# One of seven exponential-tile additions per attention step, moved from VectorE to GpSimd

## The chip, the cores and the metric

The kernel runs on one core of one Trainium2 chip. A core has a matrix engine (TensorE, "PE" in the profile, with its weight loads as "PEld"), VectorE ("DVE"), ScalarE ("ACT"), GpSimd ("POOL"), and a queue engine ("SP") that issues most of the transfers. The metric is the device time of one execution in microseconds; lower is better. Each engine works through its own instructions in order, and waits on semaphores for the results of others.

## What is computed

Two graph layers are applied to `x` of shape (16, 1024, 256), all in float32. The change lies in the softmax attention of the first layer, for 16 batches of 1024 nodes and 4 heads of 64 columns:

```python
g = relu(einsum('bcn,bnm->bcm', fea, Wg) * para)        # Wg from adj and column means
q = transpose(g).reshape(B, N, h, hd).transpose(0, 2, 1, 3)
kv = (x @ kv_w)...                                       # k, v per head
attn = softmax(einsum('bhnd,bhmd->bhnm', q, k) * scale, axis=-1)
out = einsum('bhnm,bhmd->bhnd', attn, v)
```

Around it stand layer norms, a residual sum, and a second layer (`A_hat @ features`, two linear maps with batch norms).

## The kernel before

Everything lies in `fast_path`. The order of the instructions on every engine is the order in which they are written (`tc.manual_schedule` for all five engines), so an instruction that has to wait holds up all that follows on its engine.

**The batch loop.** For each of the 16 batches `b`, TensorE does: the attention of `b`; the graph products of batch `b + 1` (`graph` for batch 1, `graph_seven` from batch 2 on, which uses seven products in place of eight); its keys and values; and the first linear map of the second layer for batch `b` (`linear1_all`). After the last batch a second stage does the other linear map, the batch norms and the output.

**One attention step.** `attention` has 4 steps per batch, 64 in all: two halves of 512 queries (`g`) by two pairs of heads (`pair`). `scores(s)` makes 8 tiles (`m` = 0..7): TensorE multiplies keys by queries into PSUM (`f_s`, L743; three such PSUM buffers), ScalarE takes the exponential into an SBUF tile `p` of 128 x 1024 floats (`f_p`, L751; 8 buffers). `values(s)` then multiplies `p` by `v` (`f_o`, L793; one PSUM bank), and VectorE moves the bank out by a transposition (L806).

**The sums of the softmax.** The denominators come from adding up the 8 tiles `p` on VectorE, in two chains: `acc` takes tiles 0, 1, 4, 6 and `flat` (the tile named `f_sums`) takes 2, 3, 5, 7. The additions in their order are L757 (`acc` = p0 + p1), **L763 (`flat` = p2 + p3)**, L766 four times (p4 to `acc`, p5 to `flat`, p6 to `acc`, p7 to `flat`), and L771 (`acc` + `flat`). These are the seven additions. Then `partial(s)` transposes `acc` into the tile of `flat` (L777) and reduces it (L785), and L806 follows after the values. In the VectorE queue the order of one step is therefore L757, L763, L766 x4, any step of `hooks`, L771, L777, L785, L806.

**What else hangs in these queues.** In steps 0 and 1 a hook makes the graph weights of the next batch: ScalarE L353 and L356, VectorE `masked` (L361). In step 2 the reciprocals of the first half are made (L826 to L829) and applied (L844). Right behind the last L806 of a batch come, on VectorE, the remaining `masked` (L361) for graph weights 2 to 7, mixed with the sums that `graph_seven` needs (L557, L561, L564, L569), the reciprocals of the second half (L826 to L829), and L844. TensorE meanwhile does the first two plain products (L514) and then the seven-product scheme (L576), of which `m2(2)` uses graph weight 7.

**Buffers.** `flat` is one buffer (tag "sums", one of one) that is also used by `graph_seven` for a loaded tile of sums; `acc` has two. The sums tile of the next step may be written only when L785 of this step has read it. GpSimd holds, in the whole kernel, the powers of the norms (L260), some DMA issues (L482, L496, L379) and sixteen small additions and products in the first batch (L1273, L1274). In the four attention steps of batch 8 it runs nothing (0.00 us).

Of the kernel before, what the change touches and what calls it, by code (L numbers as in the profile page):

```python
# [29 lines left out]
def fast_path(  # L30
# [20 lines left out]
    nc = tc.nc  # L51
# [124 lines left out]
    with ExitStack() as stage:  # L176
# [555 lines left out]
        def attention(b, qT, kT, v, hooks):  # L732

            steps = [(g, pair) for g in range(NH) for pair in range(HEADS // 2)]
            p_of, acc_of, odd_of, oT_of, o_of, red_of = {}, {}, {}, {}, {}, {}

            def scores(s, within=None, before_last=()):
                g, pair = steps[s]
                for m in range(NC):
                    ps = ps_s.tile([P, 2, 512], F32, tag="s", name=f"f_s_{b}_{s}_{m}")  # L740
                    for e in range(2):
                        rows_e = slice(e * HD, (e + 1) * HD)
                        nc.tensor.matmul(  # L743
                            ps[:, e, :],
                            kT[rows_e, pair, ts(m, P)],
                            qT[rows_e, pair, ts(g, 512)],
                            start=True,
                            stop=True,
                        )
                    p = pp.tile([P, 2, 512], F32, tag="p", name=f"f_p_{b}_{s}_{m}")  # L750
                    nc.scalar.activation(p, ps, AF.Exp)  # L751
                    p_of[s, m] = p
                    if m == 1:
                        acc = pp.tile(
                            [P, 2, 512], F32, tag="acc", name=f"f_acc_{b}_{s}", bufs=2
                        )
                        nc.vector.tensor_add(acc, p_of[s, 0], p)  # L757
                        acc_of[s] = acc
                    elif m == 3:
                        odd = ow.tile([P, 2, 16, 32], F32, tag="sums", name=f"f_sums_{b}_{s}")  # L760
                        odd_of[s] = odd
                        flat = odd.rearrange("p e j i -> p e (j i)")
                        nc.vector.tensor_add(flat, p_of[s, 2], p)  # L763
                    elif m > 3:
                        to = flat if m % 2 else acc_of[s]
                        nc.vector.tensor_add(to, to, p)  # L766
                    if m == 5 and within:
                        within()
                for step in before_last:
                    step()  # L770
                nc.vector.tensor_add(acc_of[s], acc_of[s], flat)  # L771
# [105 lines left out]
            for i in range(len(steps)):  # L877
                scores(
                    i,
                    collect if i == 2 else None,  # L880
                    [*hooks.get(i, ()), *([invert, spread] if i == 2 else [])],
                )
                partial(i)
                if i == 2:
                    scale()
                values(i)
# [1492 lines left out]
```

## Time and profile before

| what | value |
|---|---|
| three runs, median (lowest to highest) | 2392.19 us (2390.81 to 2392.27) |
| the profiled execution's own time | 2392.53 us |
| its span in the profile | 2390.7 us |
| granted TensorE clock, mean | 0.996 |
| PE busy, share of span | 2351.4 us, 98% |
| DVE busy | 1953.6 us, 82% |
| ACT busy | 1345.3 us, 56% |
| POOL busy | 174.9 us, 7% |
| one batch in the middle (from the attention of batch 8 to that of batch 9) | 130.82 us |

A row of the timeline gives the start in microseconds from the start of the span, the length, the engine, the line of the kernel, the operation, output and inputs by name, and their shapes; at its end in brackets the idle time of the engine before it, and what ended it. A row of the weight loads ("PEld") tells when TensorE took up the next operand, and on whom it waited. The sum of the lengths of VectorE's rows is a little more than the time that they take, because one addition begins while the one before is still draining: additions of 1.22 us start 1.13 to 1.14 us apart.

### The profile page before, as it was taken

The page shows a single profiled execution, that of the slowest core. Times are in us where ns is not written, and L with a number is a line of the kernel's source. Part 1 is how long each engine was busy: PE and PEld are TensorE (multiplying, and loading weights), DVE is VectorE, ACT ScalarE, POOL GpSimd, SP SyncE. Part 2 cuts the span into 40 slices and gives each one's busy share as a digit, 9 for nine tenths or more (in the row PEclk, how much of TensorE's full clock was granted, in tenths as well). Part 3 has the DMA queues.
Part 4 walks back from the last instruction along what each step waited for, and adds up shares of the span by engine and source line. Part 5 has one row for each costly group of instructions (what it writes and reads, how often), then busy time and mean ns, then how long its engine had stood idle before and what let it go on. Part 6 is the DMA issues. An engine that isn't in the chain of part 4 may idle for free.

```text
span 2390.7 us, 24368 instructions
## 1 busy us (share of the span) xinstructions
PE 2351.4 (98%) x7950; PEld 1032.3 (43%) x7950; DVE 1953.6 (82%) x2806; ACT 1345.3 (56%) x1974; POOL 174.9 (7%) x253
## 2 busy tenths in 40 slices
PE   8999999999999999999999999999999999999995
PEld 4443444434343434444343434344444434444444
DVE  6788888797979798897979797988978797757766
ACT  6846555564736455555647374555555565346653
POOL 2030010101010000101010100001010100000000
PEclk9999999999999999999999999999999999999998
DMA  5042433433342434334333424242433321355579
GB/s 189 7 144 93 142 119 123 137 118 90 99 152 68 161 93 158 102 124 136 121 99 107 141 62 163 89 167 93 138 122 123 117 83 53 114 210 181 175 238 376
DMA packets 178649, 312.44 MB, mean 131 GB/s; under 512 B 33616, under 2 KB 117072, under 8 KB 178512
## 3 DMA queue, kind: packets, MB, share of 16 engines
q1 hardware_dynamic: 164176, 267.25, 33.5%
q0 software_dynamic: 9728, 26.76, 3.7%
q10 hardware_dynamic: 4608, 16.78, 1.7%
q8 instruction: 65, 1.06, 0.2%
q14 instruction: 72, 0.59, 0.1%
HBM read 195.04 MB, written 96.79 MB: 122 GB/s over the span
## 4 chain that ended last, share of the span: by engine, by line
PE 97%; DMA 1%; DVE 1%; issue 0%; ACT 0%; SPq 0%; DVEq 0%; ACTq 0%; POOLq 0%; POOL 0%
PE f_s L743 19%; PE f_o L793 19%; PE f_aps L952 16%; PE f_zps L1058 6%; PE f_gps L576 6%; PE f_vps L450 5%; PE f_gpsx L576 5%; PE f_gps L514 4%; PE f_zx L1596 4%; PE f_zm L1596 3%; PE f_kpsx L691 2%; PE f_gps L404 2%; PE f_kps L691 2%; PE f_z2ps L1534 1%; PE f_outps L1819 1%; PE f_zps L1140 1%
## 5 line engine op out<-in xcount | busy, mean ns | idle before, releaser
L751 ACT ACTIVATE f_p<-f_s 128x1024 f32<-128x1024 f32 x512 | 477.4, 1048 | 190.3 <-PE f_s L743 190.1
L743 PE MATMUL f_s<-f_qT,f_kT 64*128 64x512 f32 x2048 | 457.2, 596 | 0.0
L793 PE MATMUL f_o<-f_p,f_v 128*64 128x512 f32 x2048 | 453.6, 595 | 0.0
L743 PEld LDWEIGHTS f_s<-f_qT,f_kT 64*128 64x128 f32 x2048 | 190.1, 185 | 264.6 <-ACT f_p L751 119.0
L793 PEld LDWEIGHTS f_o<-f_p,f_v 128*64 128x64 f32 x2048 | 141.4, 137 | 304.3 <-issue 264.4
L353 ACT ACTIVATE f_w<-f_row,f_col 128x1024 f32<-128x1024 f32 x127 | 147.0, 1157 | 38.8 <-PE f_gps L514 26.9
L766 DVE TENSOR_TENSOR f_acc<-f_acc,f_p 128x1024 f32<-128x1024 f32 x128 | 155.9, 1218 | 4.2 <-ACT f_p L751 4.2
L361 DVE SCALAR_TENSOR_TENSOR f_w<-f_w,f_adj 128x1024 f32<-128x1024 f32 x127 | 152.8, 1212 | 7.5 <-ACT f_w L356 7.3
L766 DVE TENSOR_TENSOR f_sums<-f_sums,f_p 128x1024 f32<-128x1024 f32 x128 | 155.8, 1217 | 0.0
L260 POOL TENSOR_TENSOR f_rstd_b<-f_var_b,f_mhalf 128x4 f32<-128x4 f32 (+1 forms) x31 | 33.1, 1069 | 1496.0 <-DVE f_var_b L259 1496.0
L356 ACT ACTIVATE f_w<-f_w 128x1024 f32<-128x1024 f32 x127 | 134.4, 1058 | 4.0
L952 PE MATMUL f_aps<-f_ahatT,f_hs 128*128 128x512 f32 x256 | 115.1, 592 | 0.0
L952 PE MATMUL f_aps<-f_ahatT,f_h_b 128*128 128x512 f32 x256 | 113.4, 596 | 0.0
L450 PE MATMUL f_vps<-f_kvw,f_hT 128*128 128x256 f32 x512 | 113.1, 379 | 0.0
L952 PE MATMUL f_aps<-f_t,f_hs 128*128 128x512 f32 x256 | 112.5, 592 | 0.0
L281 ACT ACTIVATE f_h_b<-f_x,f_shift_b,f_rstd_b 128x256 f32<-128x256 f32 x128 | 66.3, 592 | 75.8 <-DVE f_shift_b L266 75.6
L450 PEld LDWEIGHTS f_vps<-f_kvw,f_hT 128*128 128x128 f32 x512 | 97.3, 190 | 20.1 <-issue 7.7
L281 ACT ACTIVATE f_h_a<-f_x,f_shift_a,f_rstd_a 128x256 f32<-128x256 f32 x126 | 73.8, 587 | 50.7 <-DVE f_shift_a L266 50.7
L757 DVE TENSOR_TENSOR f_acc<-f_p,f_p 128x1024 f32<-128x1024 f32 x64 | 76.8, 1200 | 28.4 <-ACT f_p L751 28.4
L514 PE MATMUL f_gps<-f_w,f_h_a 128*128 128x512 f32 x224 | 99.9, 599 | 0.0
L763 DVE TENSOR_TENSOR f_sums<-f_p,f_p 128x1024 f32<-128x1024 f32 x64 | 78.3, 1223 | 21.8 <-ACT f_p L751 21.8
L777 DVE STREAM_TRANSPOSE f_sums<-f_acc 128x1024 f32<-128x1024 f32 x64 | 79.7, 1245 | 2.2
(278 smaller groups left out, 3607.5 us busy)
## 6 DMA issues: line engine op xcount, KB each, us to landing
f_t<-ft SPq DMA_DIRECT2D x84, 512.0 KB, 11.0
fz<-f_z SPq DMA_DIRECT2D x64, 512.0 KB, 9.7
f_x<-in_x_dram SPq DMA_DIRECT2D x31, 1024.0 KB, 7.4
f_zb<-fz SPq DMA_DIRECT2D x42, 512.0 KB, 4.2
f_att<-f_oT SPq DMA_DIRECT2D x512, 32.0 KB, 1.9
fx<-f_x SPq DMA_DIRECT2D x16, 1024.0 KB, 4.4
fhT<-f_hQ POOLq DMA_DIRECT2D x112, 128.0 KB, 2.9
f_hT<-fhT SPq DMA_DIRECT2D x28, 512.0 KB, 5.8
```

The source lines that it names most:

```text
L353: nc.scalar.activation(w, rows[b], AF.Abs, bias=cols[b][:, c : c + 1], scale=0.5 / C)
L361: nc.vector.scalar_tensor_tensor(w, w, 1.0, adj_t[c], ALU.subtract, ALU.mult)
L450: nc.tensor.matmul(ps[:, i, :], hT[e][:, ts(c4 + i, P)], kvw_t[:, e, C : 2 * C], start=(e == 0), stop=(e == CC - 1),)
L514: nc.tensor.matmul(gps[d][:, ts(g, 512)], h[:, c, ts(d, P)], w[:, ts(g, 512)], start=(c == 0), stop=(c == PLAIN - 1),)
L576: nc.tensor.matmul(ps, left, right, start=fresh and n == 0, stop=(n == PAIRS - 1), skip_group_check=more,)
L743: nc.tensor.matmul(ps[:, e, :], kT[rows_e, pair, ts(m, P)], qT[rows_e, pair, ts(g, 512)], start=True, stop=True,)
L751: nc.scalar.activation(p, ps, AF.Exp)
L766: nc.vector.tensor_add(to, to, p)
L793: nc.tensor.matmul(o_of[s][e * HD : (e + 1) * HD, :], v[:, m, ts(2 * pair + e, HD)], p[:, e, :], start=(m == 0), stop=(m == NC - 1),)
L952: nc.tensor.matmul(ps, left[:, m, :], right(m), start=not more and m == 0, stop=(m == KH - 1), skip_group_check=more,)
L1058: nc.tensor.matmul(ps[i], left[:, ts(i, P)], right, start=not more, stop=True, skip_group_check=more,)
L1596: nc.tensor.matmul(ps, left[:, m, :], right[:, m, :], start=start and m == 0, stop=(m == 1), skip_group_check=not start,)
```

## The change

In each of the 64 attention steps the addition of tiles 2 and 3 is issued on GpSimd's queue in place of VectorE's. The output tile, the operands and the four additions that follow on the two chains are the same. The L766 of `m == 5` (p5 to `flat`), which came behind L763 on the same engine, now waits for GpSimd's result.

```diff
                     elif m == 3:
                         odd = ow.tile([P, 2, 16, 32], F32, tag="sums", name=f"f_sums_{b}_{s}")
                         odd_of[s] = odd
                         flat = odd.rearrange("p e j i -> p e (j i)")
-                        nc.vector.tensor_add(flat, p_of[s, 2], p)
+                        nc.gpsimd.tensor_add(flat, p_of[s, 2], p)
```

## The prediction

> **What bounds the kernel now.** I first read the page: busy shares and the chain that ended last.
>
> ```profile
> PE 2351.4 (98%) x7950; PEld 1032.3 (43%) x7950; DVE 1953.6 (82%) x2806; ACT 1345.3 (56%) x1974; POOL 174.9 (7%) x253
> ...
> PE 97%; DMA 1%; DVE 1%; issue 0%; ACT 0%; SPq 0%; DVEq 0%; ACTq 0%; POOLq 0%; POOL 0%
> ```
>
> TensorE is the chain for 97% of the span. A busy PE could hide waits, so next the busy times by stage of one middle batch: four attention steps of batch 8, the graph products of batch 9, the rest.
>
> ```profile
> 1115.97:1172.31 56.34, 56.34 (x257) 20.75 (x257) 53.31 (x55) 41.40 (x50) 0.00 (x0) 1.00 0.21 65
> 1172.31:1197.48 25.17, 25.17 (x59) 11.13 (x60) 21.54 (x36) 10.54 (x17) 0.97 (x1) 1.00 0.75 270
> 1197.48:1246.79 49.31, 49.31 (x133) 24.09 (x131) 36.15 (x74) 21.13 (x42) 8.44 (x13) 1.00 0.32 103
> ```
>
> The columns after the length are PE, PEld, DVE, ACT, POOL, clock, DMA share and GB/s. TensorE has no gap in any stage; GpSimd does nothing in the attention; but VectorE is busy 53.31 of 56.34 us there, so it has only 3 us in hand per batch. Batches repeat every 130.82 us, and from 65.5 to 2052 us TensorE is never idle: its 39.3 us of idle time lie before the first attention (10.3) and after the last (29.3, less 0.3 of rounding). So taking work off VectorE can win nothing here; the question is only whether VectorE gets late enough to hold TensorE up. For that I read the timeline of VectorE through the last two steps of batch 8 and into the graph products, and the weight loads beside it.
>
> ```profile
> 1147.22 1.22 DVE L757 TENSOR_TENSOR f_acc<-f_p,f_p 128x1024 f32<-128x1024 f32 x1 [0.96 <-ACT f_p L751]
> 1149.05 1.23 DVE L763 TENSOR_TENSOR f_sums<-f_p,f_p 128x1024 f32<-128x1024 f32 x1 [0.61 <-ACT f_p L751]
> 1150.19 1.22 DVE L766 TENSOR_TENSOR f_acc<-f_acc,f_p 128x1024 f32<-128x1024 f32 x1
> ...
> 1161.82 1.18 DVE L757 TENSOR_TENSOR f_acc<-f_p,f_p 128x1024 f32<-128x1024 f32 x1
> 1163.19 1.22 DVE L763 TENSOR_TENSOR f_sums<-f_p,f_p 128x1024 f32<-128x1024 f32 x1 [0.19 <-ACT f_p L751]
> 1164.34 1.22 DVE L766 TENSOR_TENSOR f_acc<-f_acc,f_p 128x1024 f32<-128x1024 f32 x1
> ...
> 1172.67 0.70 DVE L806 STREAM_TRANSPOSE f_oT<-f_o 128x512 f32<-128x512 f32 x1
> ...
> 1185.94 1.22 DVE L361 SCALAR_TENSOR_TENSOR f_w<-f_w,f_adj 128x1024 f32<-128x1024 f32 x1
> ```
> ```profile
> 1187.37 0.19 PEld L576 LDWEIGHTS f_gps<-f_w,f_h_a 128*128 128x128 f32 x1 [0.24 <-DVE f_w L361]
> 1187.80 0.19 PEld L576 LDWEIGHTS f_gps<-f_w,f_h_a 128*128 128x128 f32 x1 [0.24 <-issue]
> ```
>
> From 1163.19 to 1191.7 VectorE has no idle time. The last graph weight (`masked` 7, L361) is ready at 1185.94 + 1.22 = 1187.16, and TensorE takes it up at 1187.37, for a product that begins at 1187.79. A load takes 0.19, so it could come as late as 1187.60: **about 0.4 us of slack** (0.44 less a little for the semaphore). This is the tightest place; the earlier products of L576 have 2 us or more.
>
> **What the Trainium skill says.** "SBUF — State Buffer", section "Who interferes with whom": a VectorE instruction with two SBUF inputs contends with a GpSimd instruction that reads SBUF, over a read interface that they share, and the second to issue blocks until the first is done. Both L757 and L766 have two SBUF inputs, as has the moved addition. The trace of before can't confirm it: POOL is at 0.00 us in the attention window. "GPSIMD Engine Reference", section 3.1: a float32 addition of 2048 columns takes 4497 ns on GpSimd, 2293 ns on VectorE. VectorE's 1.22 us for 1024 columns fits the latter (half is 1.15, plus a fixed part); GpSimd shows only 128 columns:
>
> ```profile
> L1273 POOL TENSOR_TENSOR f_unused_d<-f_ahatT,f_ident 128x128 f32<-128x128 f32 x8 | 4.7, 588 | 17.9 <-ACT f_unused_r L1260 17.9
> L1274 POOL TENSOR_TENSOR f_ahatT<-f_ahatT,f_ident 128x128 f32<-128x128 f32 x8 | 4.4, 546 | 0.6
> ```
>
> **The price of the moved addition, P.** Low end: half of the page's 4497 ns, 2.25 us. High end: the trace's 546 ns for 128 columns times 8, 4.4 us, which counts its fixed part eight times. Taking the page's slope (2.17 ns per column, its 2.6 cycles at 1.2 GHz) off the 546 ns leaves about 0.27 us fixed, so 2.22 + 0.27 = 2.49; I take **P = 2.4 us**, between that and 2.25.
>
> **The change, part by part.** Removed: 64 VectorE additions at a pitch of 1.135 us (the start-to-start distance around L766), 73 us of VectorE time, none of it on TensorE's path. Added: 64 GpSimd additions, on a queue with nothing else in the attention, so nothing is held up behind them; GpSimd's DMA issues (L482, L496) come in the later stage. They start when exponential 3 is there and L785 of the step before has freed `flat`; L785 is long done. Added too: the wait of L766 for p5; behind it stand all of VectorE's queue down to L806 and `masked`. Its semaphore costs nothing while P is served first, since under the lock VectorE has already been stopped for it.
>
> With the lock, L757, the GpSimd addition and the next L766 go one after another, whichever comes first; so each step costs VectorE P - 1.135 = 1.27 us more, less what idle time it swallows. Walking batch 8 (idle times from the timeline; by "late" I mean against before):
> - Step 0: no idle. The first L766, at 1123.20 before, is 1.27 late.
> - Step 1: L757 starts at 1133.20 + 1.27 = 1134.47, frees the port 1.13 later, GpSimd until 1138.0; L766 stood at 1136.11: 1.9 late (0.58 idle swallowed).
> - Step 2: L757 without its 0.96 idle at 1146.26 + 1.9 = 1148.16; GpSimd from 1149.29 to 1151.69; L766 stood at 1150.19: 1.5 late, and 1.2 after a 0.29 wait further on.
> - Step 3: L757 at 1161.82 + 1.2 = 1163.0; GpSimd from 1164.15 to 1166.55; L766 stood at 1164.34: **2.2 late**.
>
> No step delays TensorE inside the attention: `values` of step 1 needs L806 of step 0, done 3.8 us ahead; those of steps 2 and 3 have 5.0 and 3.4 us in hand. But L806 of step 3, and `masked` 7 behind it, come 2.2 late; less 0.4 of slack, TensorE stalls **1.8 us per batch**. Then VectorE catches up: at 1193.85 it waits 2.18 us for ScalarE anyway. The transfer that waits for L785 (L528, 3.6 us to landing) has some 4 us in hand.
>
> Fourteen batches (1 to 14) have this shape: 14 x 1.8 = 25.2. Batch 7 has no idle in steps 1 and 2 and ends 3.5 late: +1.3. Batch 9 has 0.36 of idle in place of 0.19 in its last step: -0.2. Batch 0: its `masked` wait 0.69, 0.90 and 0.90 us for ScalarE, which covers it: 0. Batch 15: the sum L937 ends at 2057.82 and is wanted at about 2059.0; about 1.95 late less 1.2: +0.7. Sum: **+27 us**. The profiled execution took 2392.5 (span 2390.7 plus 1.8 around it, 0.3 above the median of 2392.19): 2392.5 + 27.0 = **2419.5 us**.
>
> P counts four times in a batch: 0.1 us more of it is 0.4 x 14 = 5.6 us. P = 2.25 gives 2411, P = 2.6 gives 2431, and hand-overs at the lock count like P. If the engines share the port, so that the block is worth 2.0 us, step 3 ends 0.8 late: 14 x 0.4, about 2398.
>
> **The rivals.**
> - *No contention, and the add fits* (ends on the other side: same). VectorE gains 1.135 us in steps 0 to 2 and idles. In step 3 exponential 3 is ready at 1163.1; GpSimd would end at 1165.6, and the L766 for p5 stood at 1165.47: 0.1 to 0.2 late, under the slack of 0.4. Time 2392.5. It decides if additions on both engines overlap at full speed and P stays below about 2.7. For it: nothing in this trace shows a lock. Against: the page names this very pair of operations.
> - *No contention, but a slow add.* Then only the last step counts: late by P - 2.3, less 0.4. P = 3.3 gives 14 x 0.6, 2401; P = 4.4 gives 14 x 1.7, 2416. For it: 546 ns for 128 columns. Against: half of the page's figure.
> - *Faster.* VectorE would have to end a wait of TensorE in the attention; there is none.
>
> **How the numbers follow.** The lock, whole or partial: 0.76, most of it between 2398 and 2440. Slow add: 0.07. No contention and same: 0.14. Faster by some effect that I don't see: 0.03. A measurement tells about 0.2% (4.8 us) from no change, so faster 0.03, same 0.14, slower 0.83. The range from 2397 to 2440 takes in a weak lock and P up to about 2.75; it leaves out no change, faster, and a lock with larger hand-overs.
>
> **What would show it.** Right: VectorE's L757 or first L766 stretched to 2 to 3.5 us, or started late, beside the POOL row; L806 of step 3 about 3.3 us after TensorE's first L514 where it ended 1.1 after it before; a PE wait on L361 of about 1.8 us in 14 batches and a batch period of about 132.6 us. GpSimd's own spans are rough ("Perfetto Trace Analysis", section "GPSIMD Engine Instruction", advises against trusting them), so P is best read from when the L766 for p5 starts. Wrong: L766 at 1.22 us beside GpSimd, or a period of 130.82.

## The result, and the profile after

The changed kernel takes 2404.85 us (median of 6 runs, 2403.97 to 2405.18) against 2391.79 us before (6 runs): a ratio of 1.0054, 95% interval 1.0041 to 1.0067. It is 13 us slower; 27 had been forecast. The direction, the mechanism and the place were as predicted, the size was half.

The page of the changed kernel, with the line of busy times and the chain that ended last (profiled execution 2403.97 us, span 2402.2 us):

```profile
PE 2353.6 (98%) x7950; PEld 1031.8 (43%) x7950; DVE 1982.7 (83%) x2742; ACT 1347.2 (56%) x1974; POOL 351.4 (15%) x317
...
PE 78%; DVE 11%; issue 5%; ACT 3%; DMA 2%; SPq 1%; DVEq 0%; ACTq 0%; POOLq 0%; POOL 0%
```

VectorE has 64 instructions less and is busy 29 us *more*. The chain no longer runs through TensorE alone: it now leaves it for VectorE and ScalarE once per batch. The stages of batch 8 (columns as before: length, PE, PEld, DVE, ACT, POOL, clock, DMA share, GB/s) say where:

```profile
1121.53:1177.87 56.34, 56.34 (x257) 20.76 (x257) 53.72 (x50) 41.41 (x50) 11.13 (x4) 1.00 0.20 64
1177.87:1204.00 26.13, 25.37 (x59) 11.15 (x60) 23.02 (x37) 10.65 (x17) 1.02 (x1) 1.00 0.71 260
1204.00:1253.30 49.30, 49.30 (x132) 24.07 (x131) 36.17 (x74) 21.14 (x42) 8.43 (x13) 1.00 0.34 104
```

The attention takes 56.34 us as before, the last stage too. Only the graph products have grown, and there TensorE has its gap: 26.13 - 25.37 = 0.76 us. The table of TensorE's waits names one new cause between 190 and 2060 us, 14 times:

```profile
PE f_gps L576 <- DVE f_w L361: 10.6, 14, 0.8
```

(Three single waits of 0.3 to 0.7 us that the trace of before lacks lie outside that stretch, in the loads and in the last stage. Run 2 below, in which nothing was moved to GpSimd, has two of them as well, and in the third TensorE waits for a transfer of a weight, L1303.) The end of graph weight 7 and TensorE's rows at that place, in batch 8:

```profile
1193.00 1.22 DVE L361 SCALAR_TENSOR_TENSOR f_w<-f_w,f_adj 128x1024 f32<-128x1024 f32 x1
```
```profile
1192.50 1.02 PE L576 MATMUL f_gpsx<-f_w,f_h_a 128*128 128x512 f32 x2
1194.28 1.12 PE L576 MATMUL f_gps<-f_w,f_h_a 128*128 128x512 f32 x2 [0.76 <-DVE f_w L361]
```

This is `m2(2)`, which waits for graph weight 7. The idle time of 0.76 us understates the loss, because TensorE's rows overlap: this product begins 1.78 us behind the one ahead of it, where it began 0.86 us behind it before (1186.93 to 1187.79). From one batch's first graph product to the next the kernel now takes 131.77 us instead of 130.82: 0.95 us more in each of 14 batches, 13.3 us, which is the difference of the medians (13.1). (The two profiled spans differ by 11.5 only: this execution reached the first attention 1.06 us earlier than before's, and from the attention of batch 15 to the end it took 0.56 us less.)

Then the two engines in the attention of batch 8: VectorE in the first and the last step, and below it GpSimd in all four:

```profile
1126.50 1.21 DVE L757 TENSOR_TENSOR f_acc<-f_p,f_p 128x1024 f32<-128x1024 f32 x1
1127.82 3.20 DVE L766 TENSOR_TENSOR f_acc<-f_acc,f_p 128x1024 f32<-128x1024 f32 x1
1130.94 1.21 DVE L766 TENSOR_TENSOR f_sums<-f_sums,f_p 128x1024 f32<-128x1024 f32 x1
...
1168.13 1.18 DVE L757 TENSOR_TENSOR f_acc<-f_p,f_p 128x1024 f32<-128x1024 f32 x1
1169.67 2.95 DVE L766 TENSOR_TENSOR f_acc<-f_acc,f_p 128x1024 f32<-128x1024 f32 x1 [0.36 <-ACT f_p L751]
1172.54 1.21 DVE L766 TENSOR_TENSOR f_sums<-f_sums,f_p 128x1024 f32<-128x1024 f32 x1
```
```profile
1126.49 3.44 POOL L763 TENSOR_TENSOR f_sums<-f_p,f_p 128x1024 f32<-128x1024 f32 x1 [12.80 <-ACT f_p L751]
1140.57 2.60 POOL L763 TENSOR_TENSOR f_sums<-f_p,f_p 128x1024 f32<-128x1024 f32 x1 [10.64 <-ACT f_p L751]
1154.65 2.36 POOL L763 TENSOR_TENSOR f_sums<-f_p,f_p 128x1024 f32<-128x1024 f32 x1 [11.48 <-ACT f_p L751]
1168.80 2.73 POOL L763 TENSOR_TENSOR f_sums<-f_p,f_p 128x1024 f32<-128x1024 f32 x1 [11.79 <-ACT f_p L751]
```

GpSimd begins its row beside L757, waits for it inside its row (3.44 against 2.36 in the third step, where nothing was in its way) and ends at 1129.93. L766 begins at 1127.82 and lasts 3.20 us, to 1131.02: it is stopped until GpSimd is done and then needs 1.09 us. The same rows of step 0 before the change:

```profile
1120.94 1.21 DVE L757 TENSOR_TENSOR f_acc<-f_p,f_p 128x1024 f32<-128x1024 f32 x1
...
1124.34 1.22 DVE L766 TENSOR_TENSOR f_sums<-f_sums,f_p 128x1024 f32<-128x1024 f32 x1
```

All 64 first L766 are stretched like this (their group, with the later additions to `acc`, has a mean of 2035 ns where it had 1218). The second L766, the one that has the new semaphore to wait for, stays at 1.21 to 1.22 in every case, and begins 1.00 to 1.01 us after the end of GpSimd's row in all 64, so here the rows of the two engines fit each other.

### The profile page after: what moved, and what is told of

It is laid out like the page before. It is cut to its first block, busy times and chain, and to the rows that moved or that the text cites. A ratio compares the mean times of both kernels' runs of the same rounds, so it can differ in the third digit from the quotient of the medians.

```text
span 2402.2 us, 24383 instructions
## 1 busy us (share of the span) xinstructions
PE 2353.6 (98%) x7950; PEld 1031.8 (43%) x7950; DVE 1982.7 (83%) x2742; ACT 1347.2 (56%) x1974; POOL 351.4 (15%) x317
## 3 DMA queue, kind: packets, MB, share of 16 engines
q8 instruction: 65, 1.06, 0.2%
## 4 chain that ended last, share of the span: by engine, by line
PE 78%; DVE 11%; issue 5%; ACT 3%; DMA 2%; SPq 1%; DVEq 0%; ACTq 0%; POOLq 0%; POOL 0%
PE f_aps L952 16%; PE f_s L743 15%; PE f_o L793 14%; PE f_zps L1058 6%; PE f_vps L450 5%; PE f_zx L1596 4%; DVE f_w L361 3%; PE f_gpsx L576 3%; PE f_zm L1596 3%; PE f_gps L576 3%; ACT f_p L751 2%; PE f_kpsx L691 2%; PE f_gps L404 2%; PE f_kps L691 2%; DMA f_z<-fx 1%
## 5 line engine op out<-in xcount | busy, mean ns | idle before, releaser
L766 DVE TENSOR_TENSOR f_acc<-f_acc,f_p 128x1024 f32<-128x1024 f32 x128 | 260.5, 2035 | 41.3 <-ACT f_p L751 39.9
L763 POOL TENSOR_TENSOR f_sums<-f_p,f_p 128x1024 f32<-128x1024 f32 x64 | 175.7, 2746 | 737.8 <-ACT f_p L751 737.8
L361 DVE SCALAR_TENSOR_TENSOR f_w<-f_w,f_adj 128x1024 f32<-128x1024 f32 x127 | 152.6, 1211 | 4.0 <-ACT f_w L356 3.9
L766 DVE TENSOR_TENSOR f_sums<-f_sums,f_p 128x1024 f32<-128x1024 f32 x128 | 155.1, 1212 | 0.0
L514 PE MATMUL f_gps<-f_w,f_h_a 128*128 128x512 f32 x224 | 99.9, 599 | 0.0
L576 PE MATMUL f_gps<-f_w,f_h_a 128*128 128x512 f32 x168 | 82.7, 601 | 10.6 <-DVE f_w L361 10.6
L757 DVE TENSOR_TENSOR f_acc<-f_p,f_p 128x1024 f32<-128x1024 f32 x64 | 76.3, 1192 | 11.8 <-ACT f_p L751 11.8
```

What stands on the lines that cost most here:

```text
L361: nc.vector.scalar_tensor_tensor(w, w, 1.0, adj_t[c], ALU.subtract, ALU.mult)
L576: nc.tensor.matmul(ps, left, right, start=fresh and n == 0, stop=(n == PAIRS - 1), skip_group_check=more,)
L763: nc.gpsimd.tensor_add(flat, p_of[s, 2], p)
```

## The experiments

Theory A is the prediction's: additions on the two engines exclude each other; VectorE becomes late; at the end of the attention masked 7 is late by more than its slack, and TensorE waits there, and only there. Against it stood: the loss arises elsewhere (B); it comes from the added wait and not from contention (C); any GpSimd work stops VectorE (D). Each ratio below is to the kernel before on the same chip.

**1. L844 behind graph weight 7, in the changed kernel**, and **2. the same move in the kernel before.** Nothing else differs.

```diff
-            scale()
             masked(b, 7)
+            scale()
             m1(2)
```

Expected of the first: 

> The changed kernel, with one more move: in the graph products, L844 of the second half is issued behind masked 7 instead of ahead of it, so graph weight 7 is ready one L844 (1.13 us) earlier. Theory A (the loss is one wait per batch, of TensorE for masked 7, 0.95 us): the lateness of 1.51 us at the end of the attention stays, but no wait is left; batch period back to 130.8 us, time within 2 us of the kernel before. Rival B (the lost time arises elsewhere, and the wait at masked 7 is only where it is seen): the wait reappears at the next product that needs VectorE, period near 131.8 us, time near 2405 us.

Expected of the control: 

> The control to the run with L844 behind masked 7: the same move in the kernel before, where the addition stays on VectorE. Both theories: no wait to remove, period 130.8 us, time within 2 us of the kernel before. If this gains, the move itself is worth something and the other run may not be read as the loss undone.

Measured: 2391.04 us, ratio 1.0000 (0.9991 to 1.0008), and 2391.06 us, ratio 1.0001 (0.9993 to 1.0009). In the first, L806 of the last step still ends 2.64 us after TensorE's first graph product, as in the changed kernel (1.13 before), GpSimd and the stretched L766 are the same, and the period is 130.82 us. No wait of TensorE for another engine is left between 190 and 2060 us. So the lateness alone costs nothing, and the whole loss was the one wait for masked 7 (graph weight 7). B falls. The order gains nothing by itself.

**3. An extra addition for which nobody waits**, in the kernel before (L763 stays on VectorE; steps 0 and 1 do more work than the reference needs).

```diff
+                        if s < 2:
+                            spare = ow.tile([P, 2, 512], F32, tag="att", name=f"f_spare_{b}_{s}", bufs=1)
+                            nc.gpsimd.tensor_add(spare, p_of[s, 2], p)
                         nc.vector.tensor_add(flat, p_of[s, 2], p)
```

Expected: 

> The kernel before, with L763 left on VectorE, and in steps 0 and 1 of each batch an extra addition of tiles 2 and 3 on GpSimd into a tile that nothing reads. No instruction waits for it except the reuse of its tile much later. Theory A (a VectorE addition is stopped for the whole of a GpSimd addition, wait or no wait): L757 or L763 beside it stretch from 1.22 us to up to 3.4; VectorE is 2.2 us late after step 0, 3.4 after step 1, 1.6 after step 2 and 1.4 at the end of the attention; less 0.56 us of slack, 0.85 us per batch, so about 2404 us. Rival C (no stop, the changed kernel only loses by the added wait and the longer chain): all VectorE additions stay at 1.22 us, GpSimd's take a constant 2.4, time as before, 2392 us.

Measured: 2391.71 us, ratio 1.0004 (0.9996 to 1.0013): the 2404 of theory A missed, the 2392 of C hit. Yet the rows decide against C. Lines are three further down in this kernel, L766 is its L763 and L769 its L766. VectorE in the first step, then in the second; GpSimd's two rows below:

```profile
1121.76 1.22 DVE L766 TENSOR_TENSOR f_sums<-f_p,f_p 128x1024 f32<-128x1024 f32 x1
1122.89 1.22 DVE L769 TENSOR_TENSOR f_acc<-f_acc,f_p 128x1024 f32<-128x1024 f32 x1
...
1134.65 1.23 DVE L766 TENSOR_TENSOR f_sums<-f_p,f_p 128x1024 f32<-128x1024 f32 x1 [0.60 <-ACT f_p L751]
1135.79 3.38 DVE L769 TENSOR_TENSOR f_acc<-f_acc,f_p 128x1024 f32<-128x1024 f32 x1
```
```profile
1120.67 11.34 POOL L765 TENSOR_TENSOR f_spare<-f_p,f_p 128x1024 f32<-128x1024 f32 x1 [12.86 <-issue]
1134.76 3.33 POOL L765 TENSOR_TENSOR f_spare<-f_p,f_p 128x1024 f32<-128x1024 f32 x1 [2.75 <-ACT f_p L751]
```

In the second step an addition of VectorE is stopped from 1.22 to 3.38 us although it waits for nothing of GpSimd's: contention, not the semaphore. In the first step the reverse: VectorE has its next addition ready each time, runs eight two-input instructions in a row undisturbed to 1129.8, and GpSimd, which began at 1120.67, ends at 1132.01, 2.2 us after the first one-input instruction (a transposition) began. So step 0 cost VectorE nothing, where the expectation had put 2.2, and what step 1 cost was swallowed by the idle time of step 2: in step 3 L763 again waits 0.21 us for its exponential.

One batch of this run, batch 7, shows the loss itself without a semaphore. There L361, the seventh of the eight, had to wait for ScalarE, GpSimd got in, and VectorE was stopped in the middle of the chain:

```profile
996.48 3.13 DVE L361 SCALAR_TENSOR_TENSOR f_w<-f_w,f_adj 128x1024 f32<-128x1024 f32 x1 [0.17 <-ACT f_w L356]
```
```profile
989.47 9.06 POOL L765 TENSOR_TENSOR f_spare<-f_p,f_p 128x1024 f32<-128x1024 f32 x1 [10.90 <-ACT f_p L751]
```

GpSimd's next addition stopped the L757 that followed, to 3.18 us. L806 of the last step then ended 0.94 us later than before, TensorE waited for masked 7, and that batch took 0.38 us more than 130.82. (L361's own lateness isn't the cause: in batch 7 of the trace of before it came later still, by 2.87 us, and nothing was lost.)

**4. An extra fill that reads one column, and 5. an extra copy**, at the same place and otherwise like run 3.

```diff
+                            nc.gpsimd.tensor_copy(spare[:, 0, 0:1], p[:, 0, 0:1])
+                            nc.gpsimd.memset(spare, 1.0)
```
```diff
+                            nc.gpsimd.tensor_copy(spare, p)
```

Expected of the fill: 

> As the run with the extra addition, but GpSimd reads only one column of tile 3 (so that it starts at the same moment) and then fills the tile with a constant: it writes 1024 columns and reads none. Theory A in the form that the two engines contend for reading: VectorE's additions beside it stay at 1.22 us, time as before, 2392 us. Rival D (any GpSimd instruction of such a length stops VectorE, whatever it reads): the addition beside it is stretched by the length of the fill; with a fill of 1 to 2 us the end of the attention is up to 1.2 us late, time 2392 to 2401 us, but the stretched rows would show it in any case.

Expected of the copy: 

> The kernel before, with an extra copy of tile 3 on GpSimd in steps 0 and 1 (1024 columns read and written, one input), for which nothing waits. In step 0, where VectorE has its next two-input addition ready each time, GpSimd is expected to wait for the end of that chain as the extra addition did (11 us), and VectorE to stay at 1.22 us. In step 1, where VectorE has just run out of exponentials: if one input stops VectorE as two do, the addition beside it is stretched by the length of the copy (about 1 to 1.5 us); if only two-input instructions contend, it stays at 1.22. Time as before in both, 2391 us.

Measured: 2391.70 us, ratio 1.0003 (0.9995 to 1.0012), and 2392.06 us, ratio 1.0004 (0.9995 to 1.0013). The fill beside VectorE in the second step (GpSimd, then VectorE, whose L770 is L766 before):

```profile
1136.18 0.95 POOL L766 MEMSET f_spare<- 128x1024 f32 x1
```
```profile
1136.00 1.22 DVE L770 TENSOR_TENSOR f_acc<-f_acc,f_p 128x1024 f32<-128x1024 f32 x1
```

1024 columns written and none read leave the addition at 1.22 us, and no L770 of the run is longer than 1.23. The copy, with one input, stretches the L769 beside it to 2.06 us. D falls: in these runs it is reading that the engines don't do together, and one input on GpSimd's side is enough. In step 0 of batch 8 the row of the one-column copy lasts 9.17 us and that of the full copy 10.03 us (1.04 where nothing was in its way): both waited for VectorE's chain, like the addition of run 3.

**6. Only step 3, and 7. only steps 0 to 2 on GpSimd.**

```diff
-                        nc.vector.tensor_add(flat, p_of[s, 2], p)
+                        eng = nc.gpsimd if s == len(steps) - 1 else nc.vector
+                        eng.tensor_add(flat, p_of[s, 2], p)
```

(run 7 with `s < len(steps) - 1`.)

Expected of step 3: 

> Only step 3 of each batch makes the addition of tiles 2 and 3 on GpSimd; steps 0 to 2 leave it on VectorE. Sizes read from the trace of the changed kernel (GpSimd starts 0.12 us after exponential 3, takes 2.36 us, the L766 for p5 starts 1.01 us after its end; slack of masked 7 is 0.56 us): L766 for p5 is 1.11 us late, so is L806, stall 0.55 us per batch, period 131.4 us, about 2399 us. By the sizes of the prediction (1.08 late, slack 0.4): 0.68 us per batch, 2401 us. If the loss came from steps 0 to 2 carried over: no change, 2391 us.

Expected of steps 0 to 2: 

> Steps 0 to 2 of each batch make the addition on GpSimd, step 3 leaves it on VectorE. Sizes from the trace of the changed kernel: L757 of step 3 starts 0.75 us late, swallows 0.19 us of idle time, L806 is 0.56 us late, which is just the slack; stall 0 to 0.1 us per batch, 2391 to 2393 us. By the sizes of the prediction (1.2 late at the end of step 2, 1.0 after the idle time, slack 0.4): 0.6 us per batch, period 131.4, about 2400 us.

Measured: 2398.97 us, ratio 1.0031 (1.0019 to 1.0043), and 2391.13 us, ratio 0.9999 (0.9991 to 1.0007). TensorE's waits with step 3 alone:

```profile
PE f_gps L576 <- DVE f_w L361: 5.5, 14, 0.4
```

Both times are those worked out from the new sizes (2399 and 2391 to 2393). The 2400 that the prediction's sizes give for steps 0 to 2 is excluded. For step 3 alone their 2401 lies still within the interval (up to 2401.4), but the period decides: 0.58 us more in the trace, where they give 0.68 and the new ones 0.55. The lateness of that lone step, 1.14, is no smaller than the prediction's 1.08: there GpSimd waits for its exponential and not for L757, and it is the slack that was off. Three quarters of the moved additions cost nothing that the median shows; the quarter in the last step alone costs 60% of the loss.

**8. The first pair instead of the second.** As many additions on GpSimd, but tiles 0 and 1.

```diff
-                        nc.vector.tensor_add(acc, p_of[s, 0], p)
+                        nc.gpsimd.tensor_add(acc, p_of[s, 0], p)
```

Expected: 

> As many additions on GpSimd as in the changed kernel, but it is the one of tiles 0 and 1 (L757), which can start two exponentials earlier, when VectorE is in the one-input instructions at the end of the step before (L785, L806) or idle. Theory A (only the time that VectorE's two-input additions are stopped counts): the stop falls on the start of L763 and is about 0.6 us; L766 for p5 is 0.3 to 0.4 us late in the last step, under the slack; no stall, period 130.8 us, 2391 us. Rival (the load on GpSimd or its semaphore as such costs): as the changed kernel, 2404 us.

Measured: 2391.05 us, ratio 1.0000 (0.9991 to 1.0008). The last step of batch 8, GpSimd above, VectorE below:

```profile
1161.08 2.35 POOL L757 TENSOR_TENSOR f_acc<-f_p,f_p 128x1024 f32<-128x1024 f32 x1 [11.73 <-ACT f_p L751]
```
```profile
1162.87 1.65 DVE L763 TENSOR_TENSOR f_sums<-f_p,f_p 128x1024 f32<-128x1024 f32 x1 [1.18 <-ACT f_p L751]
1164.44 1.21 DVE L766 TENSOR_TENSOR f_acc<-f_acc,f_p 128x1024 f32<-128x1024 f32 x1
```

GpSimd starts 1.8 us ahead of VectorE's next addition, beside a transposition, and needs 2.35 to 2.37 us in all 64 cases; VectorE is stopped for 0.43 us where it was 1.4 to 2.0 in the four steps of the changed kernel. The load on GpSimd and its semaphore cost nothing; the place of the addition does. No version beats the kernel before, nor could one of this kind: TensorE has no wait there to win back.

The runs together; "late" is L806's end after the first graph product of the next batch less the 1.13 us of before, "period" is less 130.82:

| kernel | late, us | period, us | time, us |
|---|---|---|---|
| changed | 1.51 | +0.95 | +13.1 |
| only step 3 | 1.14 | +0.58 | +7.8 |
| steps 0 to 2 | 0.48 | 0.00 | 0.0 |
| first pair | 0.44 | +0.01 | -0.1 |
| changed, L844 behind weight 7 | 1.51 | 0.00 | 0.0 |

Where there is a loss, period is late less 0.56 in both cases; where late is under 0.56 there is none. Two single batches lie on the same line: batch 7 of run 3 (0.94 late, 0.38 lost) and batch 7 of run 7 (1.40 late, 0.84 lost).

## Why the prediction was half right

**What bounds the kernel, and that nothing can be gained: right.** TensorE had no wait to give back; every variant ends at 2391 us or above.

**Contention between the additions: right**, and shown by run 3 (no semaphore) and run 4 (no reading, no contention). Run 3's batch 7 has the loss itself from contention alone. The Trainium skill, "SBUF — State Buffer", section "Who interferes with whom", says so; the 3.20 us row agrees. Where that section lets the order of issue decide who waits, the trace differs: GpSimd's row of 11.34 us began before seven of the VectorE instructions that went ahead of it.

**P = 2.4 us: right.** 2.36 us undisturbed; the estimate of 2.25, half of the figure in the Trainium skill, "GPSIMD Engine Reference", section 3.1, is 0.1 too low. The value taken between the bounds stood within 0.05 us.

**The cost of a step, "P - 1.135 = 1.27 us more": the step that failed.** In the first step of batch 8 the time from L757 to the L766 for p5 was 3.40 us before (1120.94 to 1124.34) and is 4.44 now (1126.50 to 1130.94): **1.04 more, not 1.27**. The sum had 1.13 + 2.4 + 1.135 = 4.67; measured are 1.08 until GpSimd goes on (1129.93 - 2.35 = 1127.58), 2.35, and 1.01 from its end to the next start. So the pitch of two running additions was the wrong price for what follows a stop. A likely reason is that the stopped L766 has already begun, and has part of its 1.22 us behind it when it is let go: it needs 1.09 more. No run tests that.

**"P counts four times in a batch": wrong, and it follows from the same term.** Measured against the start of TensorE's step, the L766 for p5 is late by 1.04, 1.37, 1.13 and 1.51 us in steps 0 to 3, where the walk had 1.27, 1.9, 1.5 and 2.2 for the L766 before it. The idle times of steps 1 and 2 (0.6 and 1.9 us per batch) swallow all that steps 0 and 1 pile up: in step 2 L757 ends at 1154.20, GpSimd starts on its own exponential at 1154.65, and its row is the undisturbed 2.36 us. So P counted in steps 2 and 3 only. The walk also took the idle times from the brackets, which count from the end of a row, although the next addition can begin about 0.09 us before that end: the 0.29 us of step 2 swallowed 0.38 (1.13 late before it, 0.75 after). Steps 0 to 2 alone leave 0.48 at the end, step 3 alone 1.14.

**The slack, 0.4: too small, it is 0.56.** I had put a weight load of 0.19 us between the result and the product. In the trace of the changed kernel masked 7 ends at 1194.22 and the product's row begins at 1194.28, with its load, so most of that load did not come on top. Before, masked 7 was ready at 1187.16 and the product began at 1187.79: 0.63 less these 0.06 is 0.57.

Together: 1.51 - 0.56 = 0.95 instead of 2.2 - 0.4 = 1.8 per batch, 13.3 instead of 25.2. Of the 0.85 too much, 0.45 was carried into step 3 (1.2 where 0.75 was measured), 0.24 was step 3's own (1.0 against 0.76), and 0.16 was the slack. **The extras** (+1.3 for batch 7, +0.7 for batch 15) did not come in the changed kernel's trace. TensorE does not wait for the sum of batch 15 there. In batch 7 the L361 of step 0 had come 2.87 us late in the trace of before, against batch 8; in the changed kernel's it came 0.19 late. It came late in most of the other traces as well, by 0.25 to 2.4 us in runs 2 to 7, and cost 0.84 us in run 7: so it was no accident of one execution, but its size differs from one to the next, and one trace could not give it for the median.

**The rivals.** "No contention, and the add fits" is out by runs 3 and 5, "slow add" by P. The partial lock at 2398 and the slow add at 2401 gave times nearer to the measured one than the forecast did, but neither is what happened: the lock is whole and P was as taken; the walk was too dear.

## What to carry to other kernels

Moving two-input work from VectorE to GpSimd took nothing off VectorE here where VectorE's own two-input instructions ran at that moment; it did no harm where it fell on one-input instructions or idle time (run 8). That it can gain time was not shown: VectorE was not the bound. Where VectorE is not the bound, look for the one place where its result is wanted with the least slack: the loss here was late less slack, once per batch, and re-ordering two instructions there undid it whole here (run 1). A walk through four steps multiplies an error of 0.2 us in one step's price, so take that price from how an instruction behaves out of a stop, if a trace shows one, or keep the range as wide as several times that error.

## What the runs showed of the hardware that was not expected

In these runs a GpSimd instruction that reads SBUF waited as long as VectorE had its next two-input instruction ready in good time: its row was 11.34 us for an addition of 2.36, and 9.17 us for a copy of a single column. Where VectorE's next instruction came late, GpSimd got in, and VectorE was stopped until GpSimd's instruction was done. How late is late was not measured. In run 3, GpSimd was still shut out in step 0 by an L361 whose input had come 0.60 us before its start, and got in in step 1 ahead of an L769 whose input had come 0.26 us before.

The move itself seems to have opened the gap in step 0 of the changed kernel. Without L763 between them, L757 and the first L766 both write `acc`, and the second starts 0.11 us behind the end of the first, although its exponential had been there for 0.5 us; in run 3, with an addition of the other chain between them, each begins 0.08 us before the one ahead has ended, and GpSimd stays out. No run tests another order of the two chains.

GpSimd's rows contain their waiting; undisturbed they were steady here (2350 to 2368 ns over the 64 additions of run 8). A fill of 1024 columns took 952 ns and disturbed nobody.
